# A four-layer graph and expert kernel: how layer 2 fetches its gathered rows, groups its weighted sum and orders its routing

## The chip, the cores and the metric

The kernel runs on one core of one Trainium2 chip. Its time is the device time of one execution in microseconds. The core has five engines that run their own instruction streams and wait for each other by semaphores: TensorE (PE, with its weight load shown apart as PEld), VectorE (DVE), ScalarE (ACT), GpSimd (POOL) and SyncE (SP, which here only issues transfers). A profiled execution gives one line for each instruction: when it began, how long it took, and what ended the idle time before it.

## The reference, cut to what matters

Four layers work on `x` (2708 x 256, float32) with one adjacency matrix. Each layer normalises `x`, mixes rows through the matrix and adds the result, and then normalises again and adds a feed-forward part. The change lies in layer 2 and at the seams on both sides of it.

```python
    x = x + _L1_ffn_ref((_layernorm(x, axis=-1))[None], ...)[0]     # one of 8 experts for each row
    x = x + _L2_gnn_ref(_layernorm(x, axis=-1), adj, W, attn_src, attn_dst)
    x = x + _L2_ffn_ref((_layernorm(x, axis=-1))[None], ...)[0]
    x = x + _L3_gnn_ref(_layernorm(x, axis=-1), adj, ...)

    def _L2_gnn_ref(x, adj, W, attn_src, attn_dst):
        h = x @ W.T
        a_src = (h * attn_src).sum(axis=-1)
        a_dst = (h * attn_dst).sum(axis=-1)
        scores = a_src[None, :] + a_dst[:, None]
        mask = (adj > 0).astype(h.dtype)
        s = jnp.where(scores > 0, scores, ALPHA * scores) * mask
        s = s - jnp.max(s, axis=1, keepdims=True)
        e = jnp.exp(s) * mask
        w = e / (jnp.sum(e, axis=1, keepdims=True) + 1e-08)
        return jax.nn.elu(w @ h)

    def _L2_ffn_ref(x, Wr, br, W1, b1, W2, b2, gamma, beta):
        logits = jnp.mean(x, axis=1) @ Wr + br          # one choice for all rows
        routing_weights = jax.nn.softmax(logits, axis=-1)
        ...                                             # capped by a capacity, softmax again
        top_w, top_i = jax.lax.top_k(rw_tok, 2)
        top_w = jax.nn.softmax(top_w, axis=-1)
        h = jax.nn.gelu(jnp.einsum('nd,edf->enf', xf, W1) + b1[:, None, :], approximate=False)
        y = jnp.einsum('enf,efd->end', h, W2) + b2[:, None, :]
        ...                                             # weighted sum of the two experts
        return _layer_norm(out + x, gamma, beta)
```

Layer 2's experts are chosen once, from the mean of all rows, so they can't begin before the last row of the graph part is known.

## The kernel before, in words

**Tiles.** Rows are kept in SBUF as 22 tiles of 128 (`NT` = 22): tiles 0 to 20 are full (`FULL` = 21) and tile 21 has 20 rows. All is float32. A product of float32 goes through PE in two passes, so the counts of PE instructions are twice those of the products. Tile's scheduler sets the order of each engine's stream, except where the code adds an order by hand: `engine_after(first, engine, past)` puts all instructions of an engine that were emitted since `first` behind one instruction, and `in_order(first, engines)` chains those of an engine in the order in which they were emitted. `tile_pool` tiles of one name rotate through `bufs` buffers; a new one waits for the old one's last reader.

**Coming from layer 1.** The experts of layer 1 scatter their outputs by row into DRAM (`given[1]`). Tiles 0 to 7 (`EARLY`) are read back and added while layer 1 ends. The others are read at the start of layer 2, into `mine`, which has two buffers.

**The front of layer 2.** Tiles go by `FOURS`: 0-1, 2-5, 6-9, 10-13, 14-17, 18-21. `turned_up(tiles)` loads `mine` for the tiles that aren't early (L56, and L61 for the partial tile), adds it to `x` (L1585; DVE for the first four groups, POOL for 14-17 and 18-21), turns `x` on PE (L1593) and copies it out of PSUM on ACT (L1595). `valued` multiplies the turned tiles with the layer's matrix (L267), whose two extra columns give the scores. `scores_of` takes a tile `sc` (two buffers) and clears it (L1625, on DVE or POOL); ACT copies the scores into it (L1636), takes exponents of them, and DVE scales the rows into `hh` (L1646), with a column that sums the weights. `row_scores` turns the scores into rows, writes them to DRAM (L1500), `row_read` reads them back spread over all partitions into `Rb` (L1504), and ACT takes their exponent (`factors_of`).

**The weighted sum.** The loop `for n in (5, 5, 5, 4, 1, 1)` takes that many target tiles at a time. For each of the 22 source tiles j, DVE builds one block of weights `e` for the whole group (`weigh`, L1755, 128 x up to 640), and PE multiplies each target tile's 128 columns of it with `hh[:, j]` into that tile's accumulator (L1786), the 20 rows of the last source tile by `last_product` (L313). The accumulators `ps_acc` have five banks; three more are `ps_tmp`. The last two tiles (19 and 20) go one at a time; their weights `e_last` are built on DVE during the group before. After a group, `result` divides (DVE L1704, L1705, ACT L1707). What follows for each tile is put on `todo` and done during the next group: `grow` (elu and the residual, with the statistics of the new row) and `turned` (normalise on ACT L1732, turn on PE L1736, copy on ACT L1741, which also sums the columns into `xsum`). In a group they are emitted after j = 3, 5, 7, ..., in the single tiles after j = 4, 9, 14, 19.

**The choice.** The last tile (20) is finished on its own (L1828 to L1836, then `normed_by`, which is the end of `grow`). Its share is added to the mean, and DVE works out the choice: `mx`, `keys`, `over`, `rank`, `picked`, `at`, `ix` (L1851 to L1874); `ix` is read by SP to fetch the two experts' matrices. After it stand the weights `wts` (L1876 to L1891), which the bias of the experts needs (`wd` L1981, a turn L1984 and a product L1988 on PE).

**The experts and the seam to layer 3.** The experts run over six parts of the rows (`hidden` L375, `outputs` L2006). While they do, `front(own)` prepares layer 3 for the part before: turn, product (L220, L267), and at its end `row_scores`. In the last part (`end`), `at_once(scored)` ends the preparation of tiles 16 to 18. Then layer 3's weighted sum begins (L2275, L2283, weights L2246); a generator `last_stretch` does the rest of layer 2 (tiles 19 to 21) one step per source tile, from slot 1 on.

## Time and profile before

| what | us |
|---|---|
| time, median of 4 runs | 1901.22 (1897.64 to 1906.0) |
| the profiled execution's own time | 1902.64 |
| its span | 1900.8 |
| PE, DVE, ACT, POOL busy | 1822.5, 1074.6, 656.3, 389.6 |

By stage, from the busy time of each engine in stretches of the span (granted clock is that of PE, 1.00 is full speed):

| stretch, us | what runs | PE busy | DVE busy | granted clock | DMA share |
|---|---|---|---|---|---|
| 0 to 620 | layer 0 | 591.75 | 340.00 | 0.98 | 0.64 |
| 620 to 1090 | layer 1 | 447.12 | 194.89 | 0.98 | 0.51 |
| 1090 to 1120.6 | the front of layer 2 | 26.67 | 20.24 | 1.00 | 0.39 |
| 1120.6 to 1335.6 | layer 2's weighted sum | 211.50 | 115.55 | 1.00 | 0.15 |
| 1335.6 to 1348.5 | last tile and choice | 4.90 | 6.84 | 0.65 | 0.15 |
| 1348.5 to 1527.5 | layer 2's experts | 175.94 | 85.25 | 0.99 | 0.08 |
| 1527.5 to 1900.8 | layer 3 | 364.66 | 311.88 | 1.00 | 0.13 |

Matmuls are pipelined and their ends are modelled, so a busy PE may still lose time between passes; the starts of passes show it better than the busy shares. The place after which a wait is named is the one that came last by the profile.

### The profile page before, as it was taken

Reading aid. Unit: us, or ns where it says so; the run is one execution under the profiler, and the core shown is the slowest. Engines: PE = TensorE matmul, PEld = TensorE weight load, DVE = VectorE, ACT = ScalarE, POOL = GpSimd, SP = SyncE. Lnnn points to the kernel's source line nnn. Section 1 sums busy time; section 2 is a strip of 40 time slices with the busy share of each in tenths; the row PEclk is TensorE's granted clock in tenths of the full one; section 3 lists DMA queues with packets and bytes.
Section 4 is the critical chain, followed back from the end, with each engine's and each line's share of the span. In section 5 each row is a group of like instructions: output and inputs, shape, how many; then the busy total and the mean of one; then the engine's idle time right before and its main releaser. Section 6 shows DMA issues by size and latency. Waiting matters only on the chain. (4 is left out here: it accounts for less than half of the span.)

```text
span 1900.8 us, 25846 instructions
## 1 busy us (share of the span) xinstructions
PE 1822.5 (96%) x9449; PEld 1330.6 (70%) x9449; DVE 1074.6 (57%) x2469; ACT 656.3 (35%) x1475; POOL 389.6 (20%) x460
## 2 busy tenths in 40 slices
PE   8999998999998999999898999999899999999998
PEld 6888787888887888888776878887567733233344
DVE  8686861443433625354541265555254498888877
ACT  8777741222222302113231232323232552132232
POOL 0015253333322001403546320000000100011020
PEclk9999998999999999999998999999899999999999
DMA  8535655887773554544764363000101000012020
GB/s 273 153 99 165 227 185 210 332 333 267 285 285 104 176 151 127 136 125 125 217 224 129 135 101 24 1 1 1 44 1 34 12 7 24 23 26 37 23 37 18
DMA packets 92767, 231.64 MB, mean 122 GB/s; under 512 B 18223, under 2 KB 49495, under 8 KB 85208
## 3 DMA queue, kind: packets, MB, share of 16 engines
q1 hardware_dynamic: 71064, 183.28, 30.3%
q0 software_dynamic: 21568, 46.61, 8.9%
q8 instruction: 78, 1.28, 0.3%
q14 instruction: 57, 0.47, 0.1%
HBM read 218.39 MB, written 30.80 MB: 131 GB/s over the span
## 5 line engine op out<-in xcount | busy, mean ns | idle before, releaser
L2246 DVE SCALAR_TENSOR_TENSOR e<-arena,G,mask 128x1024 f32<-128x1024 f32 (+1 forms) x252 | 275.0, 1149 | 34.1 <-PE den L2283 33.2
L2275 PE MATMUL num<-e,wh 128*64 128x512 f32 (+4 forms) x1056 | 214.1, 549 | 0.3 <-DVE e L2246 0.2
L1025 PE MATMUL acc<-msg,wt 128*128 128x256 f32 x882 | 197.9, 381 | 2.8 <-DVE wt L975 1.8
L1421 PE MATMUL acc<-sup,adrow 128*128 128x256 f32 x882 | 197.9, 382 | 0.0
L1025 PEld LDWEIGHTS acc<-msg,wt 128*128 128x128 f32 x882 | 164.8, 190 | 29.0 <-DVE wt L975 3.1
L1421 PEld LDWEIGHTS acc<-sup,adrow 128*128 128x128 f32 x882 | 165.1, 190 | 27.3 <-issue 5.5
L1786 PE MATMUL ps_acc<-hh,e 128*128 128x257 f32 x798 | 179.5, 382 | 1.4 <-ACT o L1707 1.4
L649 PE MATMUL yacc<-wb,hTs 128*128 128x256 f32 x736 | 171.6, 385 | 7.8 <-DVE ys L651 7.0
L617 ACT ACTIVATE hTs<-ps_acc,wa 128x256 f32<-128x256 f32 (+1 forms) x192 | 88.8, 464 | 247.0 <-PE yacc L649 173.5
L615 PE MATMUL ps_acc<-xTs,wa 128*128 128x256 f32 (+1 forms) x768 | 170.8, 375 | 3.2 <-DVE xTs L605 3.1
L1786 PEld LDWEIGHTS ps_acc<-hh,e 128*128 128x128 f32 x798 | 148.3, 190 | 26.1 <-ACT o L1707 3.5
L615 PEld LDWEIGHTS ps_acc<-xTs,wa 128*128 128x128 f32 x768 | 137.6, 191 | 29.8 <-DVE xTs L605 6.0
L649 PEld LDWEIGHTS yacc<-wb,hTs 128*128 128x128 f32 x736 | 139.0, 193 | 27.3 <-DVE ys L651 8.1
L2275 PEld LDWEIGHTS num<-e,wh 128*64 128x64 f32 (+1 forms) x1056 | 70.3, 136 | 122.2 <-issue 105.4
L1755 DVE SCALAR_TENSOR_TENSOR e<-Rb,G,mask 128x640 f32<-128x640 f32 (+1 forms) x88 | 74.4, 847 | 77.0 <-PE ps_acc L1786 76.9
L2283 PE MATMUL den<-e,wh 128*32 128x512 f32 (+4 forms) x1056 | 112.2, 545 | 0.0
L1386 DVE TENSOR_SCALAR mask<-adrow 128x1024 uint8<-128x1024 f32 (+1 forms) x66 | 41.4, 627 | 119.5 <-DMA adrow<-in_adjT 115.5
L782 PE MATMUL yacc<-wb,hTs 128*128 128x256 f32 x384 | 92.4, 392 | 3.5 <-issue 3.2
L221 ACT COPY xT<-ps_tmp 128x256 f32<-128x256 f32 x76 | 26.7, 366 | 198.0 <-PE ps_tmp L220 197.6
L975 DVE SCALAR_TENSOR_TENSOR wt<-adrow,wt 128x640 f32<-128x640 f32 (+3 forms) x67 | 71.1, 1064 | 26.1 <-ACT wt L141 24.5
L537 POOL DMA_INDIRECT given<-ys,xs x46 | 65.3, 1420 | 94.4 <-DVE ys L652 79.9
L2283 PEld LDWEIGHTS den<-e,wh 128*32 128x32 f32 (+1 forms) x1056 | 33.1, 109 | 73.7 <-issue 69.6
(497 smaller groups left out, 2674.0 us busy)
## 6 DMA issues: line engine op xcount, KB each, us to landing
adhalf<-in_adjT SPq DMA_DIRECT2D x42, 677.0 KB
wb<-in_L_ffn_W2p SPq DMA_DIRECT2D x24, 1152.0 KB
wb<-in_L_ffn_Wdp SPq DMA_DIRECT2D x24, 1152.0 KB
wa<-in_L_ffn_W1b SPq DMA_DIRECT2D x24, 1028.0 KB
adrow<-in_adjT SPq DMA_DIRECT2D x42, 512.0 KB
adrow<-in_adjT SPq DMA_DIRECT2D x42, 320.0 KB
adrow<-in_adjT SPq DMA_DIRECT2D x21, 576.0 KB
adrow<-in_adjT SPq DMA_DIRECT2D x21, 448.0 KB
```

Source lines behind the costliest of these rows:

```text
L615: i = te.matmul(p[:, f % 2, : m * P], lhsT=w1[:, c, f * P : (f + 1) * P], rhs=xT[:, c, : m * P], start=(c == 0), stop=(c == DC - 1))
L617: s.activation(hT[:, f, : m * P], p[:, f % 2, : m * P], AF.Gelu, bias=bias[:, f : f + 1])
L649: te.matmul(q[:, k, :], lhsT=hT[:, f, k * P : (k + 1) * P], rhs=w2[:, f, :], start=(f == 0), stop=(f == HC - 1))
L782: te.matmul(q, lhsT=hT[:, f, :], rhs=w2[:, f, :], start=(f == 0), stop=(f == HC - 1))
L975: v.scalar_tensor_tensor(wt, ad, 1.0, wt, op0=ALU.is_lt, op1=ALU.mult)
L1025: te.matmul(p[:q, n - pair[0], :], lhsT=wt[:, k : k + q], rhs=msg[:r, j, :], start=(j == 0 and n == pair[0]), stop=(j == FULL - 1 and n == ...
L1421: te.matmul(p[:q, n - pair[0], :], lhsT=ad[:, k : k + q], rhs=sup[:, jj, :], start=(jj == 0 and n == pair[0]), stop=(jj == FULL - 1 and n ...
L1755: return v.scalar_tensor_tensor(e[:, :w], Rb[:, c0 : c0 + w], G[:, j, :], mask[:, j, c0 : c0 + w], op0=ALU.max, op1=ALU.mult)
L1786: te.matmul(p[:, : D + 1], lhsT=e[:, k : k + q], rhs=hh[:, j, :], start=(j == 0), stop=False)
L2246: v.scalar_tensor_tensor(e[:, :w], slow[:, m % 2, k, :w], G[:, j, 2 * pair + k, :], mask[:, j, c0 : c0 + w], op0=ALU.max, op1=ALU.mult)
L2275: te.matmul(num[k * DK : (k + 1) * DK, hf, :q], lhsT=wh[some, j, 2 * pair + k, :DK], rhs=e[some, :q], start=(j == 0), stop=(j == FULL), ti ...
L2283: te.matmul(den[z * Q : (z + 1) * Q, :q], lhsT=wh[some, i, 2 * pair + k, DK : DK + 1] .to_broadcast([some.stop - some.start, Q]), rhs=e[so ...
```

## The change

It has six parts:

1. All `mine` tiles are loaded at the head of layer 2, before anything else of the front is emitted, into four buffers; `turned_up` takes them from a dictionary. All scores go into one tile `scs`, cleared by one memset on DVE.
2. The groups of the weighted sum are 4, 4, 4, 3, 4, 1, 1. `e` is 512 columns wide at most and has five buffers in place of four of 640.
3. In the single tiles, `todo` is taken after j = 13, 15, 17, 19, and its PE instructions are put behind the product just emitted.
4. The last tile is scaled on DVE into `o` and then goes through `grow`, into which `normed_by` is merged again.
5. The choice up to `ix` is chained on DVE in the order of the code, and what follows up to `wts` is put behind `ix`.
6. The end of the preparation of tiles 16 to 18 (turn the scores, write them) is no longer done at once but as the first step of `last_stretch`.

```diff
             last_put = []
+            scs = fp.tile([P, len(FOURS), 4, 2], F32, name="sc")
+            v.memset(scs, 0.0)
+            mine = {}
+            for tiles in FOURS:
+                late = [t for t in tiles if t not in EARLY]
+                if late:
+                    mine[tiles[0]] = fp.tile([P, 4, D], F32, name="mine",
+                                             bufs=sum(q[-1] not in EARLY for q in FOURS))
+                    for i in load_tiles(nc, mine[tiles[0]], late, given[1], tiles[0]):
+                        behind(i, scattered["given1"])
...
-                if late:
-                    o = fp.tile([P, 4, D], F32, name="mine", bufs=2)
-                    for i in load_tiles(nc, o, late, given[1], t0):
-                        behind(i, scattered["given1"])
+                o = mine.get(t0)
...
-                sc = fp.tile([P, 4, 2], F32, name="sc", bufs=2)
-                (v if tiles[0] < FOURS[2][0] else g).memset(sc, 0.0)
-                return sc, []
+                return scs[:, FOURS.index(tiles)], []
...
-            for n in (5, 5, 5, 4, 1, 1):
+            for n in (4, 4, 4, 3, 4, 1, 1):
...
-                        e = gp.tile([P, 5 * P], F32, name="e", bufs=4)
+                        e = gp.tile([P, 4 * P], F32, name="e", bufs=5)
...
-                            te.matmul(p[:, : D + 1], lhsT=e[:, k : k + q], rhs=hh[:, j, :],
-                                      start=(j == 0), stop=False)
-                    if (j in (4, 9, 14, 19) if single >= 0 else j % 2 and j > 2) and todo:
+                            did = te.matmul(p[:, : D + 1], lhsT=e[:, k : k + q], rhs=hh[:, j, :],
+                                            start=(j == 0), stop=False)
+                    if single >= 0 and j in (13, 15, 17, 19) and todo:
+                        begin = len(nc.cur_bb.bb.instructions)
+                        todo.pop(0)()
+                        engine_after(begin, mybir.EngineType.PE, did.ins.name)
+                    elif single < 0 and j % 2 and j > 2 and todo:
                         todo.pop(0)()
...
-            v.scalar_tensor_tensor(rs, p[:, D : D + 1], -1.0, rowe[:, t, :], op0=ALU.mult,
-                                   op1=ALU.subtract)
+            v.tensor_tensor(rs, p[:, D : D + 1], rowe[:, t, :], ALU.add)
             v.reciprocal(rs, rs)
-            e = work.tile([P, D], F32, name="elu_e")
-            s.activation(e, p[:, :D], AF.Relu, scale=rs)
-            lnexp(e, e, AF.Exp, scale=-1.0)
             o = gp.tile([P, D], F32, name="o", bufs=6)
-            v.tensor_scalar(o, p[:, :D], rs, 0.0, op0=ALU.mult, op1=ALU.min)
-            v.tensor_tensor(x[:, t, :], x[:, t, :], o, ALU.subtract)
-            normed_by(t, P, e)
+            v.tensor_scalar(o, p[:, :D], rs, None, op0=ALU.mult)
+            grow(t, P, o)
...
+            choice = len(nc.cur_bb.bb.instructions)
             mx = gp.tile([P, 1], F32, name="mx")
...
             v.tensor_copy(ix, at[:, :, 0])
+            in_order(choice, (mybir.EngineType.DVE,))
+            choice = nc.cur_bb.bb.instructions[-1].name, len(nc.cur_bb.bb.instructions)
...
             v.tensor_tensor(wts[:, 1, :], wts[:, 1, :], wts[:, 0, :], ALU.mult)
+            engine_after(choice[1], mybir.EngineType.DVE, choice[0])
             turned(t, P)
...
                     scored = front(was[0])
                     for _ in range(len(was[0]) + 1):
                         next(scored)
-                    if end:
-                        at_once(scored)
...
                 own = was[0]
+                yield from scored
                 yield from finish(*was, True)
```

More of the change, by code (lines that the diff above doesn't have):

```diff
@@ L1715, in grow @@
                 v.scalar_tensor_tensor(x[:q, t, :], o, 0.0, x[:q, t, :], op0=ALU.max, op1=ALU.add)
-                normed_by(t, q, e)
-            def normed_by(t, q, e):
                 v.scalar_tensor_tensor(x[:q, t, :], e, -1.0, x[:q, t, :], op0=ALU.add, op1=ALU.add)
```

## The prediction

> **What bounds the kernel now.** I read the busy shares first: TensorE (PE) is busy 96% of 1900.8 us, and the table by stage puts 211.50 of 215 us in the weighted sum of layer 2 (1120.6 to 1335.6). So a part of the change is worth only what PE stands still for, or what work it drops. The diff drops no PE work. I therefore looked for PE's gaps inside layer 2, in the chain of waits and in PE's own timeline.
>
> The chain of waits between 1088 and 1126 us (start, length, what):
>
> ```profile
> 1094.23 2.87 DMA mine<-given
> ...
> 1097.85 5.37 DMA mine<-given
> ...
> 1103.29 2.50 POOL x L1585 x2
> 1105.79 3.30 issue
> ...
> 1110.33 0.11 POOL sc L1625
> 1110.47 0.26 ACT sc L1636
> ```
>
> The gathered rows (`mine`) of tiles 14 to 17 come after a buffer is freed, those of 18 to 21 after another; POOL adds them, and a small memset of `sc` sits on POOL behind an add that waits for the last load. The DMA queue of SP in order shows the same from the other side:
>
> ```profile
> 1094.23 0.88 SPq L56 DMA_DIRECT2D mine<-given  x2
> 1095.22 0.34 SPq L1500 DMA_DIRECT2D rows<-L_gnn_W  x1
> 1097.85 0.37 SPq L56 DMA_DIRECT2D mine<-given  x1
> 1099.54 0.34 SPq L1504 DMA_DIRECT2D Rb<-rows  x1
> 1105.82 0.36 SPq L56 DMA_DIRECT2D mine<-given  x1
> 1106.74 0.27 SPq L1500 DMA_DIRECT2D rows<-L_gnn_W  x1
> ```
>
> From 1099.54 to 1105.82 SP issues nothing, so the second write of `rows` waits behind the fourth load. PE's timeline at the change of a group of five tiles, and through the two single tiles (start, duration, line, tiles, count of passes, idle before):
>
> ```profile
> 1221.84 1.13 PE L313 MATMUL ps_acc<-hh,e 20*128 20x257 f32 x10
> 1223.71 9.25 PE L1786 MATMUL ps_acc<-hh,e 128*128 128x257 f32 x40 [0.75 <-ACT o L1707]
> ...
> 1312.12 5.05 PE L1786 MATMUL ps_acc<-hh,e_last 128*128 128x257 f32 x22
> 1318.40 0.33 PE L1736 MATMUL ps_tmp<-ident,xn 128*128 128x128 f32 x1 [1.23 <-ACT xn L1732]
> ...
> 1324.14 0.70 PE L313 MATMUL ps_acc<-hh,e_last 20*128 20x257 f32 x2
> ```
>
> A product takes two passes; ten passes take 2.165 us (from one `e` to the next on DVE, 1161.28, 1163.44, 1165.61), so one is 0.2165 us.
>
> **Gathered rows in four buffers, scores zeroed once.** Before, DVE finishes adding tiles 10 to 13 at 1101.98, but the fourth load goes out at 1105.82 and lands near 1109.1, when POOL resumes. After, all five transfers (256, 512, 512, 384 and 20 KB) are issued from 1094.23 on, 0.4 us each. I expect no gain on the third load: between 1098 and 1102 the DMA share is 0.95 to 1.00, so it is already behind the second's data and POOL still starts near 1103.3. Then come 404 KB more at the 327 to 330 GB/s of that stretch, 1.3 us, so the fourth lands near 1104.6 and POOL takes it straight after tiles 14 to 17, at 1105.8 instead of 1109.1: 1.3 + 1.4 us of adds end at 1108.5 instead of 1111.8. The ACT copies of scores that waited 2.91 us for `sc` on POOL go at once, and so do the `hh` rows on DVE that free the PSUM banks. PE then: it still waits 1.8 us for the add of 14 and 15 (to 1104.6) and ends the products of 10 to 13 at 1109.67 as now. From there it has turns of 18 to 21 (8 passes, about 1.1), products of 14 to 21 (2 x 3.5) and a little score turning (0.5), 8.6 us without a stall: 1118.3 against 1120.58 for the first weighted product. That is **-2.3**. Bounds: all PE work left from 1104.6 is 12.7 us (turns 1.7, products 10.4, scores 0.6), which ends at 1117.3 (-3.3); with the 1.8 us wait also filled by products of 10 to 13, -5; nothing at all if ACT or DVE stalls it as now (0). The two memsets on DVE (65 ns each) become one of 48 values, and four on POOL go.
>
> What is late next is `rows`: its first 2 KB write now stands on SP behind three more loads, at 1096.3 instead of 1095.22. The write took 4.3 us with two loads ahead (1095.22 to 1099.54) and 1.5 with none (1110.89 to 1112.42). I take a landing with the loads, at 1104, its read back at 1107, and the second write and read (now 1106.74 and 1109.43) some 1 to 3 us earlier than now because SP no longer stops at 1099.54. `e` starts at 1114.32 now, so the weights stay ahead of PE.
>
> [...]
>
> **Groups of four.** Five accumulators and five banks leave no spare: in the two clean changes (1221.84 and 1271.19) the ten last passes take 1.06 and then PE loses 0.75 + 0.42 us and 0.69 + 0.57 us, because every first product waits for a result to leave its bank. With 0.75 at the first change (7.47 us from 1167.67 to 1175.14, of which 6.7 is work) that is 3.2 us. After, with four, one bank is free: the last passes end 0.85 after they begin, the free bank takes 0.43, and the first result is out 1.82 after (1221.84 to 1223.66), or 1.65 as an `e` of 512 columns holds DVE 0.14 less. So 0.4 us is lost at each of three changes, none at 3 to 4 tiles and none into the single tile (as now, 0): 1.3. That is **-1.9**; bounds -3.2 and 0. DVE pays: 66 x 0.885 + 22 x 0.745 = 74.4 us of `e` becomes 88 x 0.745 + 22 x about 0.61 (halfway between 256 columns, 0.478, and 512) = 79.0. The 4.6 us lie under PE, for which DVE waits 76.9 us there. Without that cover they would cost 4.6.
>
> **Turns later in the single tiles.** Tile 19: 1312.12 to 1324.14 is 12.02 us; 42 passes (9.1) and 7 turns of 0.11 are 9.9, so 2.1 is lost, 1.23 of it where the first turn waits for `xn`. Tile 20 loses 1.1 likewise. Put behind j = 13, 15, 17, 19 (1318.2, then about 1.3 apart), turns meet `xn` that was ready at 1318.35, 1318.85, 1320.55 and 1321.72. Behind each waiting turn stand the products of its tile; I leave 1.0 us of small waits, as ACT needs about 1.5 us for one tile (xn 0.6, two copies of 0.46). **-2.3**; bounds -3.2 (no wait) and 0 (both turns of a tile back to back, 0.6 each for five tiles).
>
> **Last tile on DVE.** Now from the reciprocal's end (1336.02) to the statistics at 1338.24 is 2.22 us, as DVE waits 0.60 for ACT's read of the same bank. After: `o` on DVE 0.48, then relu, exp, add of 0.45 each, as for tile 19 (1325.40 to 1327.25 = 1.85): 1.9 to 2.0. **-0.2**, bounds -0.3 and +0.2.
>
> **Choice in order.** The three small operations that now stand between `keys` and `ix` (1343.09, 1343.41, 1344.05) fill gaps between dependent ones, so `ix` gains at most 0.1. But the weights behind it start at 1344.24 instead of 1343.09, and 1.05 us goes into `wd`, whose turn PE does ahead of the experts' first product:
>
> ```profile
> 1346.62 0.37 PE L1984 MATMUL ps_tmp<-ident,wd 128*8 128x128 f32 x1 [3.55 <-DVE wd L1981]
> 1347.36 1.22 PE L1988 MATMUL ps_tmp<-b,wT 8*128 8x256 f32 x2 [0.37 <-DVE wT L1986]
> 1348.51 11.95 PE L375 MATMUL ps_tmp<-arena,w 128*128 128x512 f32 x22
> ```
>
> Bounds: +1.05 if that order stays, 0 if the products are put first, as their weights land near 1348.4. I take **+0.7**. The granted clock is 0.50 from 1340 to 1352 and full from 1354. [...]
>
> **Scores of 16 to 18 moved into layer 3.** One turn (0.27) and its 0.92 us of waiting leave the gap before 1527.49, and the turn, a copy (0.25) and a write on SP come back one product later, where nothing reads them before the third stretch. But `e` on DVE runs without a break from 1522.90 and PE waits for it at 1543.8 to 1550 anyway, so an earlier start is mostly eaten. **-0.2**, bounds -0.9 and +0.3.
>
> **Sum.** -2.3 - 1.9 - 2.3 - 0.2 + 0.7 - 0.2 = -6.2 us. The profiled execution took 1902.64 (span 1900.8): 1896.4. The runs' median, 1901.22, is 1.4 lower: **1895.0**.
>
> **Rivals.** *More in the front:* the products of 10 to 13 move ahead of the turn that waits for POOL (another -2 to -2.7), and layer 3 keeps its 0.9: about 1891.5. For it: their copies are ready at 1103.3. Against: the order on PE is set by what is emitted first, and that is the turn. *The stall only moves:* ACT or DVE keeps PE to 1120.6 and half of the boundary gain stays away: -3, 1898.5. For it: ACT waited for `Rb` at 1115.97. *Slower, ACT held by `Rb`:* ACT's exponent of the first `Rb` stands at 1103.65, ahead of the copy of turned tiles 14 and 15 (1105.30). If the write of `rows` is as late as its queue is long, 4.3 x 1684/768 = 9.5 us, it lands at 1105.8; the read takes 4.1 as now, to 1109.9, 6.2 later than now; with 1.2 us of slack, ACT and PE lose 5. If the second `Rb` holds ACT too (1.5 + 3.5 us later), up to 10. With the -3.9 of the other parts, 1902 to 1907, say 1905. It decides when the first `Rb` lands after about 1105. Against it: transfers then ran at over 300 GB/s, not at the mean of those 4.3 us.
>
> **How the numbers follow.** Forecast 0.55 (own range 1892 to 1898.5), more 0.17, moved 0.16, slower 0.12. What this kernel's measurement can tell from no change is about 0.3%, 5.7 us: below 1895.5 or above 1906.9. Forecast gives 0.33 below and 0.22 within; more is below; moved is within; of slower 0.02 is within. So faster 0.50, same 0.40, slower 0.10. The range runs from the further gain to the edge of the slower case: 1889.5 to 1902.
>
> **What would show it.** Five `mine` issues in a row on SP; POOL's adds ending near 1108.5; the first weighted product at 1118 (before 1117 speaks for more, after 1120 for moved, after 1122 with ACT waiting for `Rb` for slower); under 0.5 us lost at each change of group; tile 19 in about 10.5 us; the stretch from the last weighted product to the experts' first (1335.6 to 1348.51 now, 12.9 us) at about 13.4, with `wd` a microsecond later behind `ix`. I am wrong if layer 3's long stretch or a layer before moves by more than 2 us.

## The result and the profile after

The changed kernel is **slower**: median 1907.95 us (36 runs) against 1902.07 (57 runs of the kernel before), ratio 1.0039 with a 95% interval of 1.0028 to 1.0049. Forecast were 1895.0 and a gain.

The profiled execution of the changed kernel is its fastest (1900.14 us, span 1898.1), so the two spans can't be set against each other. Layers 0 and 1 are the same program in both, yet layer 1's last product starts at 1089.4 us before and at 1081.0 after; in the other profiles of this study that point lies anywhere from 1064 to 1096. I therefore count from that point, between the starts of passes that both traces have: layer 1's last product, the first weighted product, the first product of the single tiles, the last weighted product, the first product of the experts, layer 3's first `num` product, the end.

| stage of layers 2 and 3 | before, us | after, us | difference | forecast |
|---|---|---|---|---|
| front | 31.2 | 34.5 | +3.4 | -2.3 |
| groups | 191.5 | 191.9 | +0.4 | -1.9 |
| single tiles | 23.1 | 21.9 | -1.3 | -2.3 |
| choice of experts (last tile included) | 13.2 | 13.8 | +0.6 | +0.7 - 0.2 |
| experts | 179.0 | 178.8 | -0.2 | 0 |
| layer 3's long stretch | 373.3 | 376.2 | +2.9 | -0.2 |
| from layer 1's end to the end | 811.4 | 817.1 | +5.7 | -6.2 |

The +5.7 agrees with the medians' +5.9. The stages are of one profile each. In the profiles below, kernels with the same code in a stage agree within 0.1 us in the groups and within 0.15 in layer 3; the front, the choice and the experts' stage scatter by up to 2.7, 0.6 and 1.8 us.

Two stages make the loss. PE's timeline at the head of the front before (start, duration, line, tiles, count), and ACT's:

```profile
1089.65 1.47 PE L1593 MATMUL ps_tmp<-ident,x 128*128 128x128 f32 x12
1090.96 2.42 PE L267 MATMUL ps_acc<-w_l,xT 128*128 128x258 f32 x10
```

```profile
1090.29 1.56 ACT L1595 COPY xT<-ps_tmp 128x512 f32<-128x512 f32 x3 [3.98 <-PE ps_tmp L1593]
```

PE's timeline in the front of the changed kernel (in brackets the idle time before and what ended it):

```profile
1081.26 1.47 PE L1600 MATMUL ps_tmp<-ident,x 128*128 128x128 f32 x12
1087.23 4.67 PE L267 MATMUL ps_acc<-w_l,xT 128*128 128x258 f32 x10 [4.50 <-ACT xT L1602]
1091.70 0.32 PE L1497 MATMUL ps_tmp<-ident,sc 128*2 128x128 f32 x1
...
1100.37 0.65 PE L1600 MATMUL ps_tmp<-ident,x 128*128 128x128 f32 x4 [0.81 <-DVE x L1592]
1101.51 0.66 PE L1600 MATMUL ps_tmp<-ident,x 128*128 128x128 f32 x4 [0.48 <-DVE mv L189]
```

The first products of layer 2 wait 4.50 us, and then ten passes take 4.67 us, at a granted clock of 0.50 (from 1085 to 1091 us); before, the same ten began 1.3 us after the first turn and took 2.42, at a clock of 1.00. ACT, whose copy PE waits for, in the changed kernel:

```profile
1086.60 1.56 ACT L1602 COPY xT<-ps_tmp 128x512 f32<-128x512 f32 x3 [8.68 <-DMA L_ffn_br<-in_L_ffn_br]
```

The turns had been done for 3.9 us when the copy started; before, it started 0.64 us after the first turn and waited for PE alone. The queues of POOL and SP in the changed kernel, in order of time:

```profile
1083.52 1.01 POOL L537 DMA_INDIRECT given<-xn,names  x1 [0.30 <-issue]
1084.51 0.62 POOL L121 DMA_DIRECT2D L_ffn_br<-in_L_ffn_br  x1
```

```profile
1085.91 2.23 SPq L56 DMA_DIRECT2D mine<-given  x4
1088.18 1.12 SPq L61 DMA_DIRECT2D mine<-given  x1
1092.33 0.24 SPq L1500 DMA_DIRECT2D rows<-L_gnn_W  x1
1096.25 0.36 SPq L1504 DMA_DIRECT2D Rb<-rows  x1
```

Layer 1's last scatter (`given<-xn,names`) is issued at 1083.52; the `mine` loads, which wait for the scatters, go out at 1085.91, and the copy of turned columns starts only 0.7 us after them. So a copy that needs nothing of the scatters waits as long as they do. The five loads go out in one piece, as forecast. POOL's adds were forecast to begin no later than before, but they run from 1096.03 to 1102.03, 15.0 to 21.0 us after layer 1's last product, against 13.9 (1103.29) to 22.4 before.

The second loss lies in layer 3, and all of it in the first of its turns: from the first `num` product to the copy that ends that turn 66.2 us before, 69.1 after, and every later turn is as long as before. DVE there, first before, then after:

```profile
1522.90 9.64 DVE L2246 SCALAR_TENSOR_TENSOR e<-arena,G,mask 128x1024 f32<-128x1024 f32 x8
1532.47 0.41 DVE L193 BATCH_NORM_STATS2 st<-y 128x6 f32<-128x256 f32 x1
```

```profile
1517.59 9.64 DVE L2249 SCALAR_TENSOR_TENSOR e<-arena,G,mask 128x1024 f32<-128x1024 f32 x8
1528.77 2.48 DVE L2249 SCALAR_TENSOR_TENSOR e<-arena,G,mask 128x1024 f32<-128x1024 f32 x2 [1.54 <-issue]
1531.17 0.42 DVE L193 BATCH_NORM_STATS2 st<-y 128x6 f32<-128x256 f32 x1
```

`e` has eight buffers. After eight, DVE did the statistics of the last tiles (1.6 us, 1532.47 to 1534.06) while the `den` products freed buffers; now the statistics stand behind the ninth and tenth `e`, and DVE idles 1.54 us in front of these. The profile names no releaser for this wait; that it is the buffer is read from PE, whose first `den` products begin at 1527.59:

```profile
1527.59 2.78 PE L2286 MATMUL den<-e,wh 128*32 128x512 f32 x24
```

PE and ACT in the same stretch of the changed kernel:

```profile
1553.92 1.16 PE L267 MATMUL ps_tmp<-w_l,xT 128*128 128x264 f32 x4 [1.56 <-ACT xT L221]
```

```profile
1550.67 1.99 ACT L141 ACTIVATE arena<-arena 128x1024 f32<-128x1024 f32 x2
1552.56 1.05 ACT L2165 ACTIVATE wh<-wh 128x64 f32<-128x64 f32 x4
1553.52 0.35 ACT L221 COPY xT<-ps_tmp 128x256 f32<-128x256 f32 x1
```

The copy that PE waits for stands behind the exponent of the next turn (1.99 us) and four scalings; before, the copy came ahead of the exponent:

```profile
1552.91 0.35 ACT L221 COPY xT<-ps_tmp 128x256 f32<-128x256 f32 x1
1553.16 2.00 ACT L141 ACTIVATE arena<-arena 128x1024 f32<-128x1024 f32 x2
```

At two changes of group, and behind them, PE's timeline of the changed kernel:

```profile
1197.98 0.72 PE L313 MATMUL ps_acc<-hh,e 20*128 20x257 f32 x8
1198.63 0.70 PE L1787 MATMUL ps_acc<-hh,e 128*128 128x257 f32 x2
1199.73 7.01 PE L1787 MATMUL ps_acc<-hh,e 128*128 128x257 f32 x30 [0.40 <-ACT o L1712]
...
1208.14 0.33 PE L1737 MATMUL ps_tmp<-ident,xn 128*128 128x128 f32 x1 [0.43 <-ACT arena L1742]
...
1239.40 5.04 PE L1787 MATMUL ps_acc<-hh,e 128*128 128x257 f32 x22 [0.36 <-ACT o L1712]
...
1246.09 0.33 PE L1737 MATMUL ps_tmp<-ident,xn 128*128 128x128 f32 x1 [0.67 <-ACT arena L1742]
...
1315.80 0.44 PE L1737 MATMUL ps_tmp<-ident,xn 128*128 128x128 f32 x2 [0.83 <-ACT arena L1742]
```

The changes lose 0.40 and 0.36 us, as forecast (0.4). New are waits at the turns of normalized tiles, 0.43 and 0.67 us: the second turn of a tile waits for ACT's copy of the first. In the single tiles (last line) 0.83 us is left of such a wait.

### The profile page after: what moved, and what is told of

It reads as the page before. It is cut to its first block, busy times and chain, and to the rows that moved or that the text cites. A ratio compares the mean times of both kernels' runs of the same rounds, so it can differ in the third digit from the quotient of the medians.

```text
span 1898.1 us, 25861 instructions
## 1 busy us (share of the span) xinstructions
PE 1820.2 (96%) x9449; PEld 1330.0 (70%) x9449; DVE 1080.9 (57%) x2490; ACT 657.3 (35%) x1475; POOL 388.7 (20%) x456
## 5 line engine op out<-in xcount | busy, mean ns | idle before, releaser
L2249 DVE SCALAR_TENSOR_TENSOR e<-arena,G,mask 128x1024 f32<-128x1024 f32 (+1 forms) x252 | 275.1, 1149 | 36.7 <-PE den L2286 34.2
L649 PE MATMUL yacc<-wb,hTs 128*128 128x256 f32 x736 | 170.5, 383 | 7.7 <-DVE ys L651 7.0
L1756 DVE SCALAR_TENSOR_TENSOR e<-Rb,G,mask 128x512 f32<-128x512 f32 (+1 forms) x110 | 79.1, 720 | 70.6 <-PE ps_acc L1787 70.5
L782 PE MATMUL yacc<-wb,hTs 128*128 128x256 f32 x384 | 89.3, 385 | 4.0 <-issue 3.9
```

Of the source, the lines that this page charges most:

```text
L649: te.matmul(q[:, k, :], lhsT=hT[:, f, k * P : (k + 1) * P], rhs=w2[:, f, :], start=(f == 0), stop=(f == HC - 1))
L782: te.matmul(q, lhsT=hT[:, f, :], rhs=w2[:, f, :], start=(f == 0), stop=(f == HC - 1))
L1756: return v.scalar_tensor_tensor(e[:, :w], Rb[:, c0 : c0 + w], G[:, j, :], mask[:, j, c0 : c0 + w], op0=ALU.max, op1=ALU.mult)
L2249: v.scalar_tensor_tensor(e[:, :w], slow[:, m % 2, k, :w], G[:, j, 2 * pair + k, :], mask[:, j, c0 : c0 + w], op0=ALU.max, op1=ALU.mult)
```

## Experiments

My theory after the traces: (1) the new order of creation in the front's pool put `xT4` over layer 1's row indices (`names`) and its gathered rows (`hs`), so the first copy has to wait for the scatters that read them, and PE's clock falls meanwhile (to 0.50, for 6.8 us); (2) the scores of tiles 16 to 18, as a step of their own, move everything behind them in layer 3's hand-written order by one product. By the addresses that the build gave, `xT4` stood at bytes 204384 to 212576 of a partition before and stands at 220960 to 229152 now; `names` is at 224832. Each stage can be read by itself, so several kernels carry edits in more than one stage. "Front" and the like are the stages of the table above.

### e1_place, e2_seam, e3_both: each cause undone, and both

```diff
 e1_place (on the changed kernel)
+            first_xT = [fp.tile([P, DC, W], F32, name="xT4", bufs=2)]
             scs = fp.tile([P, len(FOURS), 4, 2], F32, name="sc")
...
-                xT = fp.tile([P, DC, W], F32, name="xT4", bufs=2)
+                xT = first_xT.pop() if first_xT else fp.tile([P, DC, W], F32, name="xT4", bufs=2)
 e2_seam (on the changed kernel)
                         next(scored)
+                    if end:
+                        at_once(scored)
...
-                yield from scored
 e3_both: the two together
```

> The changed kernel with one difference: the first buffer of turned columns (`xT4`) is created ahead of `sc` and the four `mine` buffers, so it stands where it stood before the change and no longer over layer 1's row indices. Theory (the first copy waits for layer 1's scatters only because of this place, and PE falls to the half clock meanwhile): the first copy starts within 1 us of the first turn, PE's first product of layer 2 has no wait of 4.5 us and no half clock, and the stretch from layer 1's last product to the first weighted product is 28.9 us or a little less (34.6 in the changed kernel, 31.2 before). Layer 3 stays at 376.2. Median some 5.7 us below the changed kernel's 1907.95: 1902. Rival (the five early loads or the late write of `rows` hold the front): the stretch stays above 33 us, median 1908.

> The changed kernel with only the turn and write of the scores of tiles 16 to 18 put back ahead of layer 3's long stretch. Theory (the extra step moves everything in that stretch one product later; DVE then waits 1.54 us for a buffer of `e` with the statistics queued behind, and PE 1.56 us behind an exponent on ACT): the stretch from layer 3's first weighted product to the end goes from 376.2 back to 373.3 us, the front stays at 34.6, median 1905. Rival (layer 3 is slower for another reason, its placement or what runs ahead of it): it stays at 376 and the one turn in front of it costs 0.9 on top, median 1909.

> Both of the above in one kernel. Theory (the two causes are separate and explain the whole loss and more): front 28.9, layer 3 373.3, so 8.6 us below the changed kernel: 1899.4, and 2.5 us below the kernel before. Rival (one of them is not the cause, or what is freed is lost at the next place): 1904 to 1908.

| | front | layer 3 | from layer 1's end | median; ratio to before (95%) |
|---|---|---|---|---|
| e1_place | 30.5 | 376.1 | 813.9 | 1905.81; 1.0014 (0.9994 to 1.0033) |
| e2_seam | 34.6 | 373.3 | 814.7 | 1908.49; 1.0027 (1.0011 to 1.0043) |
| e3_both | 32.1 | 373.3 | 811.9 | 1905.11; 1.0009 (0.9994 to 1.0024) |

The kernel before had 1902.6 in these runs. The medians came out 3.5 to 5.7 us above what I had expected, and the ratio of e2_seam can't be told from the changed kernel's 1.0039 (1.0028 to 1.0049); the stages carry the argument. Layer 3 went back to 373.3 exactly when the step was undone, and the wait of 4.50 us is gone where `xT4` is back. But the front came to 30.5 and 32.1, not to 28.9, and e3_both is not faster than before. In e1_place PE now waits later on, in its timeline:

```profile
1106.41 1.26 PE L1601 MATMUL ps_tmp<-ident,x 128*128 128x128 f32 x8 [1.27 <-DVE x L1593]
1107.51 0.27 PE L1497 MATMUL ps_tmp<-ident,sc 128*4 128x128 f32 x1
1108.89 1.11 PE L1601 MATMUL ps_tmp<-ident,x 128*128 128x128 f32 x4 [1.11 <-POOL x L1593]
```

and its clock falls there; the table by stretch of e1_place (busy us of PE, PEld, DVE, ACT, POOL, then granted clock, DMA share, GB/s):

```profile
1105.00:1107.00 2.00, 0.73 (x5) 0.42 (x4) 1.33 (x4) 0.92 (x6) 0.00 (x0) 1.00 1.02 339
1107.00:1109.00 2.00, 0.89 (x7) 0.58 (x7) 2.00 (x10) 1.32 (x3) 1.43 (x2) 0.82 0.33 110
1109.00:1111.00 2.00, 2.00 (x8) 1.71 (x9) 2.00 (x8) 0.00 (x0) 2.00 (x2) 0.50 0.19 67
```

PE works 0.73 and 0.89 of 2 us, and what follows runs at 0.50. In e3_both, with the same front, the clock was low for 6.8 us, twice the 3.4 of e1_place. ACT also stands: 2.69 us for the first `Rb` in e1_place, 3.10 in e3_both. So a second thing holds the front, which the wait for the scatters had hidden: while the changed kernel waited, its loads arrived (DVE's adds of tiles 10 to 13 at 1098.79 wait for no transfer).

### e4_pad: the place alone, in the kernel before

```diff
             last_put = []
+            first_o = [fp.tile([P, 4, D], F32, name="mine", bufs=2)]
+            pad = fp.tile([P, 8 * D], F32, name="pad")
+            g.memset(pad[:, :1], 0.0)
...
-                    o = fp.tile([P, 4, D], F32, name="mine", bufs=2)
+                    o = first_o.pop() if first_o else fp.tile([P, 4, D], F32, name="mine", bufs=2)
```

> The kernel before with nothing changed but the place of `xT4`: the two `mine` buffers and an unused block of 8 KB per partition are created first, which puts `xT4` where the change puts it. Loads, their order and their buffers are as before. Theory: the first copy of turned columns waits for layer 1's scatters here too, PE's first products run at the half clock, and the front grows from 31.2 by 4 to 6 us; all other stages as before; median 1906 to 1908. Rival (place is no matter, the loads are): 31.2 and 1902.

Front 34.2 (+3.0), all later stages as before (191.5, 23.1, 13.1, 179.3, 373.3), median 1909.26, ratio 1.0035 (1.0018 to 1.0051). PE's timeline has the same wait to the digit:

```profile
1092.87 1.47 PE L1596 MATMUL ps_tmp<-ident,x 128*128 128x128 f32 x12
1098.84 4.67 PE L267 MATMUL ps_acc<-w_l,xT 128*128 128x258 f32 x10 [4.50 <-ACT xT L1598]
```

So the place makes this wait, without any of the loads moved. The front grows by less than the 4 to 6 us expected: the delay of 4.7 us (the first product starts 5.97 after the first turn, not 1.31) and the 2.25 us that the ten passes lose to the half clock (granted 0.50) are partly won back, because rows have arrived meanwhile. PE's later waits above 0.2 us in the front come to 0.75 us here, where they came to 3.65 before. Which of the things under `xT4` is waited for isn't told apart: the profile names a small load on POOL's queue, issued 1 us after the last scatter.

### e7_stats, e8_merge, e12_five: layer 3's two waits, and the turns in the groups

```diff
 e7_stats (on e1_place)
-                yield from scored
-                yield from finish(*was, True)
+                fin = finish(*was, True)
+                yield next(fin)
+                yield from scored
+                yield from fin
 e8_merge (on e1_place)
-                yield from scored
                 yield from finish(*was, True)
+                at_once(scored)
...
-                    elif single < 0 and j % 2 and j > 2 and todo:
+                    elif single < 0 and j % 2 and j > 6 and todo:
 e12_five (on the kernel before, groups of five)
-                    if (j in (4, 9, 14, 19) if single >= 0 else j % 2 and j > 2) and todo:
+                    if (j in (4, 9, 14, 19) if single >= 0 else j % 2 and j > 6) and todo:
```

> The changed kernel with `xT4` in its old place, and in layer 3 the statistics of the last tiles put ahead of the moved scores, so that DVE has its 1.54 us of statistics at the same product as before and only what follows them moves one product later. Theory (two waits of 1.5 us make layer 3's 2.9: DVE's for a buffer of `e`, and PE's for a copy of turned tiles behind an exponent on ACT): the first goes and the second stays, layer 3 374.4 to 375.2 us. Rival (the whole loss comes from the first wait): 373.3. Rival (from the turn of scores alone): 376.2.

> The changed kernel with `xT4` in its old place and two differences in separate stages. In layer 3 the moved scores share a step with the last step before the turns of tiles 19 to 21, so that they take no step of their own. Theory: nothing else moves to a later product and layer 3's long stretch is 373.3 to 373.8 us (rival, the turn itself is the cost: 376). In the weighted sum the turns of normalized tiles start at the eighth instead of the fourth source tile. Theory (the 1.3 us that the groups of four lose at turns come from results that are not yet ready, as a group of four reaches its first turn sooner): the groups take 190.4 to 190.9 us (191.9 in the changed kernel, 191.5 before). Rival (ACT as a whole is later, wherever the turns stand): 191.9.

> The kernel before, with groups of five, and only the turns of normalized tiles in the weighted sum begun at the eighth instead of the fourth source tile. Theory (before, these turns lost only 0.45 us, and the rest of the loss was at the changes of group, which groups of four take away): groups 191.0 to 191.3 us against 191.5, so the 190.0 of the run with groups of four comes from the groups. Rival (the gain is that of later turns alone): 190.0. The other stages as before, with a second look at the front (31.2 in the one profile of before) and whether its clock falls.

Layer 3: e7_stats 374.5, e8_merge 373.5. With the statistics back at their product 1.7 of the 2.9 us are gone; the rest stays, and with it one wait in the timeline of e7_stats's PE:

```profile
1535.14 1.16 PE L267 MATMUL ps_tmp<-w_l,xT 128*128 128x264 f32 x4 [1.56 <-ACT xT L221]
```

So both waits count, and the scores' turn itself costs next to nothing: merged into another step, it leaves 0.2 us.

Groups: 191.5 before, 191.9 in the changed kernel, 190.0 in e8_merge, 190.9 in e12_five. Later turns alone are worth 0.6 us with groups of five; the groups of four give a further 0.9 once the turns are later, and without that they lose 0.4. The rival (later turns are all of it) falls, and so does my expectation of 191.0 to 191.3, narrowly. (Four kernels have one run each: e7_stats took 1881.01 us, e8_merge 1874.47 and e6_lag, below, 1881.25, where the kernel before had a median of 1875.7 on that chip, and e12_five took 1894.64 against 1901.6 on another. A single time can't show a difference of this size; these four are read by stage.) e12_five is also a second profile of the front before: 30.6, no fall of the clock.

### e5_in_place, e6_lag, e10_own, e11_all: what still holds the front

```diff
 e5_in_place (on the kernel before, xT4 created first, sc zeroed once)
-                    o = fp.tile([P, 4, D], F32, name="mine", bufs=2)
+                    o = fp.tile([P, 4, D], F32, name="mine", bufs=4)
 e6_lag (on e3_both)
-                for f in factor:
-                    factors_of(f)
-                factor = [Rb[:, t0 * P : (t0 + n) * P]]
+                if len(factor) > 1:
+                    factors_of(factor.pop(0))
+                factor.append(Rb[:, t0 * P : (t0 + n) * P])
...
 e10_own (as e5_in_place, but with)
+                    o = (fp.tile([P, 4, D], F32, name="mine_last") if tiles[-1] == FULL else
+                         fp.tile([P, 4, D], F32, name="mine", bufs=2))
 e11_all: e9_best (below) with the loads as in e10_own
```

> The kernel before with four `mine` buffers instead of two and `sc` zeroed once, but with each load issued at its old place in the program, so the first write of `rows` stands behind two loads and the first read of `Rb` behind three; `xT4` is first in its place in memory. All else as before. Theory (with `xT4` moved back the front still loses, because the five loads all stand ahead of the first `rows` write: in the two kernels with it moved back ACT waits 2.7 and 3.1 us for `Rb` at 1111, PE waits behind it and falls to half clock): here `Rb` comes in time and the front is 28.5 to 29.5 us, median 1900. Rival (more bytes under way early are what delays the rows of tiles 10 to 15, whatever the order): 30.5 to 32, median 1902.

> The kernel with both repairs (front 32.1 us, layer 3 373.3), with one more difference: ACT's exponent of each `Rb` is issued one group later, so that the first no longer stands ahead of the copies of turned tiles 14 to 17. The loads stay early. Theory (ACT held by `Rb` makes the loss that is left in the front): no wait of ACT for `Rb` above 1 us ahead of these copies, clock 1.0 throughout, front 29 to 30 us. Rival (the loads arrive too late for the adds of tiles 10 to 15 on DVE and POOL, 1.0 to 1.5 us each, and that is the loss): front above 30.5.

> The kernel before with one buffer more, for the last of the four loads alone, and `sc` zeroed once; loads at their old places in the program, so the third still waits for a free buffer and the first two have the transfers for themselves. Theory (the four transfers at once make the rows of tiles 10 to 13 some 1 us later, PE's waits then fall together within 5 us and the clock halves, which eats the gain; only the last load's wait was worth taking away): no wait of PE for the DVE adds above 0.3 us, no fall of the clock, front 28.5 to 29.4 us. Rival (what is gained at tiles 18 to 21 is lost to the late `Rb` or to the clock anyway): 30.2 to 31.5.

> The kernel without the fixed order of the choice, with the loads at their old places and one buffer more for the last load alone in place of the five early loads. Theory: front 28.5 to 29.4, groups 190.0, singles 21.9, choice 13.0, layer 3 373.5; from layer 1's end 806.5 us against 811.4 before: ratio 0.9975. Rival (the front's gain depends on chance falls of the clock): 808 to 809, ratio 0.9985.

| | front | longest waits of PE in it | clock at half for |
|---|---|---|---|
| e5_in_place | 30.2 | 0.99 DVE, 1.12 POOL | 3.4 us |
| e6_lag | 30.8 | 0.60 and 0.68 DVE, 1.20 POOL | 3.4 us |
| e10_own | 32.7 | 1.20 DVE, 3.34 POOL | 3.4 us |
| e11_all | 33.2 | 0.87 DVE, 4.06 POOL | 3.4 us |

Ratios: e5_in_place 0.9991 (0.9981 to 1.0002), e10_own 1.0020 (0.9997 to 1.0042), e11_all 1.0001 (0.9989 to 1.0014), with 810.8 us from layer 1's end. None of the four expectations held; e6_lag came out where its rival had it. In e5_in_place the first write of `rows` stands behind three of the five loads, not behind two, and `Rb` is read 13.2 us after layer 1's last product, against 14.7 in e1_place and 10.1 before, so the test is weaker than meant. ACT waits 1.70 us for it instead of 2.69, and the front, with the same 3.4 us of half clock, is only 0.3 shorter than in e1_place. ACT's wait for the first `Rb` is no matter either (e6_lag: the exponent is out of the way, and the front is no shorter than the 30.5 to 30.8 of the kernels that lose the same 3.4 us). e10_own doesn't test what it was meant to: SP's queue shows the last load ahead of the third, which still waits for a buffer:

```profile
1085.25 0.88 SPq L56 DMA_DIRECT2D mine<-given  x2
1086.31 0.38 SPq L56 DMA_DIRECT2D mine_last<-given  x1
...
1088.86 0.39 SPq L56 DMA_DIRECT2D mine<-given  x1
```

The rows of tiles 14 to 17 then come behind those of 18 to 21, and PE gets to the turn of tiles 14 and 15 17.7 us after layer 1's end (1080.4 to 1098.14), against 15.2 before and 15.6 with all five loads at once in e1_place. A last load of its own behind the third, where it stood, wasn't tried.

### e9_best, e13_later, e14_later_lag: the choice of experts, and PE's order in the front

```diff
 e9_best (on e8_merge: the order of the choice taken out)
-            choice = len(nc.cur_bb.bb.instructions)
...
-            in_order(choice, (mybir.EngineType.DVE,))
-            choice = nc.cur_bb.bb.instructions[-1].name, len(nc.cur_bb.bb.instructions)
...
-            engine_after(choice[1], mybir.EngineType.DVE, choice[0])
 e13_later (on e9_best)
-                while todo and len(ahead) < 2:
+                while todo and len(ahead) < 2 and (todo[0] != FOURS[4] or not ahead):
+                    done, at = last_of(fronts), len(nc.cur_bb.bb.instructions)
                     ahead.append(turned_up(todo.pop(0)))
-                    if len(ahead) == 1:
+                    if ahead[-1][0] == FOURS[4]:
+                        engine_after(at, mybir.EngineType.PE, done[mybir.EngineType.PE])
+                    if k == 0 and len(ahead) == 1:
 e14_later_lag: e13_later with the edit of e6_lag
```

> The changed kernel with `xT4` in its old place, the moved scores merged into another step, the turns in the weighted sum from the eighth source tile on (as in the run before), and now without the fixed order of the choice of experts; the last tile is still scaled on DVE. Theory (the order costs about 0.7 us because the weights of the experts start later, the last tile on DVE gains 0.2): the stretch from the last weighted product to the experts' first is 12.9 to 13.1 us, where the kernels with the order have 13.6 to 14.3 and those before the change 13.1 to 13.3; groups 190.0, singles 21.9, layer 3 373.5 as in the run before. Front 29.4 without a fall of the clock, 30.5 to 32 with one. From layer 1's end 808 us, 3 us under the kernel before: ratio 0.998 to 0.9985. Rival (the longer choice comes from elsewhere, the last tile on DVE): 13.6 or more.

> The best version so far (ratio 0.9966) with one difference: in the front PE's turns of tiles 14 to 21 stand behind the products of tiles 10 to 13, not ahead of them. Theory (the early loads gain less than forecast because PE waits 1.1 to 1.5 us for POOL's add of tiles 14 and 15 with ready products queued behind, next to 1.0 to 1.3 us for DVE's adds, and this idle stretch lets the clock halve for 3 to 4 us): the wait on POOL is gone or under 0.5 us, no fall of the clock in the front, front 27 to 28.5 us against 30.7; others unchanged, so from layer 1's end 805 to 806, ratio 0.995 to 0.996. Rival (ACT, held by the first `Rb` ahead of the copies, is what makes PE stand): front 30 to 31 and PE waits for ACT or the clock falls as before.

> The same with ACT's exponent of each `Rb` issued one group later. Theory (PE's order is the cause, ACT's wait for `Rb` has slack): the front is within 0.5 us of the run without this. Rival (ACT held by `Rb`): 1 us or more shorter than that one.

| | front | groups | singles | choice | layer 3 | from layer 1's end | median; ratio to before (95%) |
|---|---|---|---|---|---|---|---|
| e9_best | 30.8 | 190.0 | 21.9 | 12.7 | 373.5 | 808.4 | 1896.35; 0.9966 (0.9947 to 0.9984) |
| e13_later | 29.2 | 190.0 | 21.9 | 13.2 | 373.5 | 805.8 | 1899.02; 0.9966 (0.9947 to 0.9986) |
| e14_later_lag | 29.0 | 190.0 | 21.9 | 13.2 | 373.5 | 805.8 | 1900.25; 0.9977 (0.9961 to 0.9994) |

The kernel before had 1901.6 beside e9_best and 1904.57 beside the other two. All three beat the kernel before by the interval, and so, by the ratios, the changed one; among themselves the ratios can't tell them apart. That e13_later and e14_later_lag came to 805.8, as expected, is in part luck: 1.3 to 1.6 us of their step from e9_best's 808.4 lie in the experts' stage (178.0 and 178.3 against 179.5), whose code is the same. The order of the choice: PE's wait for `wd` in e8_merge and then in e9_best:

```profile
1318.26 0.37 PE L1989 MATMUL ps_tmp<-ident,wd 128*8 128x128 f32 x1 [4.53 <-DVE wd L1986]
```

```profile
1336.04 0.37 PE L1985 MATMUL ps_tmp<-ident,wd 128*8 128x128 f32 x1 [3.55 <-DVE wd L1982]
```

0.98 us of wait are the order's: the wait is 4.53 or 4.54 us in every kernel with the order and 3.54 to 3.56 in every one without. Of the stage it is 0.9 us in this pair (13.7 against 12.7); e13_later and e14_later_lag, without the order, took 13.2. In e13_later products of tiles 10 to 13 stand where PE waited for POOL:

```profile
1107.29 1.26 PE L1601 MATMUL ps_tmp<-ident,x 128*128 128x128 f32 x8 [1.32 <-DVE x L1593]
1108.38 0.51 PE L1497 MATMUL ps_tmp<-ident,sc 128*4 128x128 f32 x2
1108.73 4.01 PE L267 MATMUL ps_acc<-w_l,xT 128*128 128x258 f32 x16
1112.58 1.63 PE L1601 MATMUL ps_tmp<-ident,x 128*128 128x128 f32 x12
1114.87 0.64 PE L1601 MATMUL ps_tmp<-ident,x 128*128 128x128 f32 x4 [0.66 <-ACT xT L1603]
```

The wait on POOL is gone, the clock stays at 1.00 through the whole front, and the front is 1.6 us shorter, though not the 2.2 to 3.7 I had expected. ACT waits for `Rb` as long as ever in e13_later (2.71 us), and taking this away (e14_later_lag) is worth 0.2. So ACT's wait had slack.

How much of the 1.6 is the order's own? The front of e7_stats has the old order and lost nothing to the clock, and it took 29.5 us. At full clock the new order is therefore worth 0.3 (between single profiles on two chips), and the rest is the fall that didn't come. PE's longest waits in the front of e7_stats were of the usual size, 0.89 us for DVE and 1.52 for POOL, so these waits do not bring a fall each time. By the traces, PE was busy 0.00 to 0.51 of the 3.4 us ahead of each fall in these fronts. In the three fronts with the old order and no fall (before, e12_five, e7_stats) the emptiest 3.4 us have 0.40 to 0.43, in e13_later and e14_later_lag 0.61 and 0.66. That fits the theory that the new order takes away the stretch in which the clock can fall; two profiles don't show that it never falls. The wait of 1.32 us for DVE's adds is left, and no kernel here takes it away.

## Why the prediction was wrong, step by step

**The step that failed first** is the first sentence on the front's end: "Before, DVE finishes adding tiles 10 to 13 at 1101.98, but the fourth load goes out at 1105.82", and from there "-2.3". The working starts in the middle of the front and takes all that lies before it as unchanged. I did follow the tiles' loads and memsets to their new places in the program, but not the tiles themselves to their new places in memory. What came in its place: a delay of 4.7 us, and 2.25 us lost to the half clock, ahead of everything that the step reckons with (e1_place and e4_pad show it from both sides). From the end of those ten passes to the first weighted product it is 27.28 us before (1093.30 to 1120.58) and 23.88 after (1091.70 to 1115.58), so what the step did reckon with came out at -3.4, just past the -3.3 that it gave for PE's work alone. That is luck: the rows arrived during the wait. In e7_stats, without that wait, the same stretch took 25.62 (1071.72 to 1097.34), -1.7.

**The -2.3 without that wait** was too much as well. With `xT4` back, the same front took 30.5, 32.1, 29.5, 30.7 and 30.8 us in five profiles (e1_place, e3_both, e7_stats, e8_merge, e9_best). The 29.5 is the one without a fall of the clock, -1.7 against the 31.2 of before and -1.1 against the 30.6 of e12_five; the others lose to the clock what was gained. At full clock the last part of the working holds: from the turn of tiles 14 and 15 to the first weighted product it has 13.7 us (1104.6 to 1118.3), and e7_stats took 13.91 (1083.43 to 1097.34). The step said that PE "still waits 1.8 us" and "From there it has ... 8.6 us without a stall". That the third load gains nothing was right: PE gets to the turn of tiles 14 and 15 15.6 us after layer 1's end in e1_place, 15.2 before. But in front of it PE now waits 1.27 us for DVE where it waited 0.22: with five transfers at once DVE's adds of tiles 10 to 13 start 12.4 us after layer 1's last product (1105.67 in e1_place) instead of 11.3 (1100.69), which the step didn't price. The two waits together are the idle stretch at whose end the clock fell in four of these five profiles. The rival "more in the front" named the remedy that e13_later carries out, and the reason against it ("the order on PE is set by what is emitted first, and that is the turn") held until it was changed.

**Slower, ACT held by `Rb`** was right about direction and wrong about cause; that its 1905 lies near the measured 1907.95 is luck. In the changed kernel the write of `rows` took 3.92 us (issued at 1092.33, 6.4 us after the first of the five loads), not the 9.5 that this rival had estimated; `Rb` was read from 1096.25 on and its exponent ran at 1102.84 without a wait. Where ACT did wait 2.5 to 3.1 us, taking the wait away gained 0.2 us (e14_later_lag) or, among fronts with the same 3.4 us of half clock, nothing (e6_lag).

**Groups of four, -1.9.** The losses at the changes are as worked out (0.40, 0.36). The term that was left out is the turns: a group of four reaches its first turn after 6.84 us (1199.73 to 1206.57) and the group of three after 4.88 (1239.40 to 1244.28), where one of five took 9.09 (1223.71 to 1232.80), and ACT isn't ready. Moved to the eighth source tile, they leave 190.0, that is -1.5. Of this 0.6 is the later turns' own (e12_five), so the smaller groups by themselves gave 0.9, half of what was forecast. (In the working, 66 x 0.885 + 22 x 0.745 is 74.8 and not 74.4; nothing in the sum rests on it.)

**Turns later in the single tiles, -2.3**: -1.3. Tile 19 took 11.29 us (1307.49 to 1318.78) against 12.02 before and about 10.5 forecast. Mechanism right, size off: I left 1.0 us of small waits for tile 19 and 20 together, and the one of tile 19 alone is 0.83.

**Last tile on DVE, -0.2**: from `rs` to the statistics 2.58 us before (1335.66 to 1338.24) and 2.54 after (1329.76 to 1332.30), so nothing: the last add took 0.70 us there, where the forecast went by tile 19's 0.45. **Choice in order, +0.7**: the wait for `wd` grew by 0.99, and the stage by 0.9 in the one pair whose code differs in nothing else (e8_merge, e9_best); over all kernels whose clock was low for 13.7 us there, 13.7 to 14.0 with the order and 12.7 to 13.2 without. In the choice the clock was low for 13.7 us before and after. In e1_place, e6_lag and e7_stats, the same program there, it was low for 17.1 and the stage took 14.2 instead of 13.7 to 14.0; in e5_in_place and e10_own, with the choice as before, it was low for 17.1 too and the stage took 13.3, where before took 13.2. So 3.4 us more of low clock were worth 0 to 0.6 in this stage.

**Scores moved into layer 3, -0.2 with bounds -0.9 and +0.3**: +2.9, the second large miss. The step counted the turn, the copy and the write, and said "come back one product later, where nothing reads them". It did not count what the step displaces: in an order written out by hand, a step of its own moves every later step by one product, past a buffer wait on DVE and past an exponent on ACT. The forecast had named the sign of it: "I am wrong if layer 3's long stretch ... moves by more than 2 us".

## What to carry to other kernels

Where a change creates tiles earlier or in another order, find out what each tile of that pool now lies on, and who still reads that: a wait can appear at an instruction that the diff doesn't touch. Where an order is written out by steps, an added step is paid by everything behind it; put new work into an existing step, and look at what stands next to what on each engine afterwards. And a gain that sits behind another wait may show only while that wait is there: undo one cause at a time, and read each stage by itself.

## What the runs showed of the hardware

**Half clock in portions.** Summed over windows of 1 us, the granted clock of the front was low for 3.4 us in e1_place, e5_in_place, e6_lag, e8_merge, e9_best, e10_own and e11_all, and for 6.8 us in the changed kernel, e2_seam, e3_both and e4_pad; in the other five it was never low, and there is nothing in between. Kernels with the same front had none (e7_stats), one (e1_place) or two portions (e3_both). With them one and the same front spreads over 2.7 us (29.5 to 32.1), while the groups of kernels with the same loop agree within 0.1.

**DVE and POOL adding side by side.** In the changed kernel two adds of 128x512 on DVE take 2.66 us while POOL adds too, and in e1_place 1.29 with POOL idle; POOL's five adds take 6.00 us there and 5.10 in e1_place.

```profile
1098.79 2.66 DVE L1592 TENSOR_TENSOR x<-x,mine 128x512 f32<-128x512 f32 x2
```

```profile
1105.67 1.29 DVE L1593 TENSOR_TENSOR x<-x,mine 128x512 f32<-128x512 f32 x2 [1.22 <-DMA mine<-given]
```
